# Graph attention on one Trainium2 core: value blocks of three batches in the setup and the rest in batch 3, a value step moved, narrow flag and input-sum products

## The chip, the cores and the metric

The kernel runs on one core of a Trainium2 chip. The core has five engines that run side by side, each with a stream of instructions of its own: TensorE (PE in the profile, its weight loads PEld) multiplies matrices, VectorE (DVE), ScalarE (ACT) and GpSimd (POOL) work on elements, SyncE (SP) does nothing here but issue transfers. The metric is the time of one execution on the device in microseconds (us); less is better.

## The reference

One layer of graph attention with 16 batches (B), 512 rows each (N), 512 features (F), 16 heads of 32 and 20 keys (the first 20 rows). All is float32. Cut to what matters:

```python
row_zero = v.sum(-1) == 0
q_exp = jnp.where(row_zero[..., None], 0.0, q[:, None, :])
self_feat = concatenate([v, q_exp], -1) @ W_self.T + b_self      # (16, 512, 512)
output = self_feat
for d in range(2):
    A = adj if d == 0 else swapaxes(adj, 1, 2)                   # (16, 512, 512, 11) int
    A = A[:, :, :20]
    cond, vb = A.sum(-1), A @ w_bias + b_bias
    kv = self_feat[:, :20]
    qh = (self_feat @ Wq[d].T + bq[d]).reshape(B, N, 16, 32)
    kh = (kv @ Wk[d].T + bk[d]).reshape(B, 20, 16, 32)
    aff = einsum('bnhd,bmhd->bnhm', qh, kh) / sqrt(32)
    w = softmax(where(cond[:, :, None] > 0, aff, -9e15) + vb[:, :, None])
    out_t = einsum('bnhm,bmf->bnhf', w, kv)
    output = output + (einsum('bnhf,hgf->bnhg', out_t, Wout[d]) + bout[d]).reshape(B, N, F)
out = v + relu(output)
```

## The kernel before, in words

The order of the instructions on every engine is the order in which they are written: the kernel turns the automatic scheduler off and interleaves the work by hand. Tiles come from pools; a new tile of a pool waits until the one that held its place is done with.

**What is computed.** The query projection is folded into the keys: for each key row and head the kernel makes one vector over the 512 features, so that the scores of a tile of 128 rows and all 16 heads, two directions and 19 keys (key 0 is taken off the others) are a product of the row features with 608 columns. In the same way the output weights are folded into the values ("vw": for each batch 20 rows by 512 for each direction). The weighted sum then needs the values of four heads laid out in blocks, zero outside, so that one product does several heads.

**Setup (lines 458 to 786).** In this order:
- All loads are issued at once, most on SP's queue in the order of lines 511 to 529 (`wo_sb`, the output weights, come after the first `x`, line 527), the first ones on ACT's.
- `kv_terms` (line 537): the features of the 20 key rows of all batches, 320 columns, as the sum over four chunks k of the input for each of four chunks fc of features: 16 products 128 x 128 x 320 (`ps_kv`). The first two rounds of k are written ahead of the products with `q` (line 547), the third and fourth behind them. A product with `ones` over a sum of the inputs gives the flags of zero rows of the keys (line 555).
- `key_rows` (line 589): the 304 columns of key differences `kvD` by the key weights, eight groups (d, jc), each over four chunks k as four products of 32 outputs (line 596), one for each quarter of the 128 output partitions. The first four groups come ahead of the bursts, the others with the first bursts. DVE adds the bias (line 602), into `khD`.
- Twenty **bursts** (line 745). A burst makes the folded keys (`keys`, line 672) for 26 or 25 units; its products (line 681) go to a pair of PSUM tiles from `ps_s`, of which there are two, so each burst waits until ACT (line 696) and DVE (line 698) have read the one before. Finished stages are written to DRAM (`g_d`, `g1_d`, lines 703 and 704) and read back per batch.
- Between the bursts stand fillers from a table (`plan`, line 726): each word is the list of fillers behind one burst, counted from the burst at which the key rows are all made. `m` is a bias term, `v` a value step, `w` a value step of the last 64 rows, `b` and `c` biases, `n` the flags of zero rows of batches 0 and 1 (`row_flags`, line 211: one product of 128 x 128 ones with 512 columns), `p` one of the seven block products for the features of batch 0. Ahead of burst n = 4 stands one value step outside the table (line 749).
- A **value step** (`values`, line 645) is one chunk k of the product of key features with output weights: for the first 256 rows (t = 0, 1) four products of 32 outputs over 512 columns. Behind the fourth chunk DVE copies the sum out (line 660) and POOL issues transfers to `vw_d` in DRAM (line 664), split at batch `EARLY` into two parts of their own.
- `bd_d`, also in DRAM in two parts, holds the **value blocks**. Part 0 is zeroed by one transfer on POOL's queue (`clear_first`, line 145), part 1 by eight on SP's (`clear_rest`, line 153, issued in batches 0 to 2 at the places `clears(b)`). Then `blocks` (line 161) lists twelve transfers for each part, each of which copies runs of 128 bytes from `vw_d` to `bd_d`, and `spill(n, queue)` (line 184) issues the next n of them. Part 0: six on POOL's queue behind the late bursts (line 774), six in batch 0 (line 871).

**The loop (line 806).** For each batch b four tiles nt of 128 rows. Per tile: `scores` (line 349, products at line 365) on TensorE; `weigh` (DVE: add, maximum, subtract, lines 379 to 387); `expo` (ACT, line 392); in the next tile `normal` (DVE sum and reciprocal, lines 415 and 416, POOL product, line 417) and `turn` (DVE, line 424). In the third tile of batch b the weighted sum of batch b - 1 is made (`attend`, line 435, `ps_o`), with its values loaded from `bd_d` in tile 0 (`load_values`, lines 137 and 850), and DVE, ACT and POOL finish it (lines 441 to 449).

Beside that the next batch is prepared: its features by seven block products (`product`, line 250; DVE puts the parts together in `partial`, line 285, and `joined`, line 297), differences of its inputs on POOL (`x_sum`, line 233), masks (ACT lines 317 and 337, DVE line 328, POOL line 344), and the sums of rows (`row_sum`, line 189, on ACT, tile 3 of batch b for batch b + 2), from which come the flags of zero rows (`nz`). Block products 4 and 3 of batch b come in its own tile 0, around the scores: the first half of these scores (k = 0, 1, line 837) stands ahead of `partial(b, 1, 0)` on DVE, the second half (k = 2, 3, line 844) behind it.

**SP's queue.** SP issues nearly all loads of the loop, in written order: `load_x` (107), `load_xn` (113), `load_adj` (119), `load_cq` (124), `load_keys` (135), `load_values` (141), `load_nz` (202), the stores (454). Most are held back until a named instruction of another engine is done (`behind`, line 97), so that a pool's place is free and loads come in turn. Part 1 of the value blocks is copied from here: four places in a batch, each with `spill(1)` in batches 3, 4 and 5 (lines 856, 877, 909, 932): behind the mask load of tile 0, behind `x_sum` 1 and its mask load, behind `x_sum` 2 in tile 1, and in tile 2 behind two pieces of `load_xn` and ahead of the last (line 939).

Of the kernel before, what the change touches and what calls it, by code (L numbers as in the profile page):

```python
# [13 lines left out]
P = 128  # L14
# [4 lines left out]
def gat_kernel(  # L19
# [20 lines left out]
    nc = tc.nc  # L40
# [42 lines left out]
    cq_d = dram.tile([B, H, 2, NG], F32, name="cq_d")  # L83
    EARLY = 5
    parts_of = ((0, EARLY), (EARLY, B))
# [98 lines left out]
    def spill(n, queue=nc.sync):  # L184

        for _ in range(n):
            queue.dma_start(*copies.pop(0))
# [23 lines left out]
    def row_flags(b):  # L211
        ps = bank(f"ps_nz{b}")
        nc.tensor.matmul(ps[:, :N], ones, rss[b], start=True, stop=True)  # L213
        nzs[b] = load.tile([P, N], F32, tag="nz", name=f"nz{b}")
        nc.vector.tensor_scalar(nzs[b], ps[:, :N], 0.0, None, ALU.not_equal)
# [242 lines left out]
    with tc.tile_pool(name="setup", bufs=1) as sp, tc.tile_pool(name="ps_acc", bufs=4, space=PSUM) as acc["pool"]:  # L458
# [19 lines left out]
        with tc.tile_pool(name="setup_k", bufs=1) as sk:  # L478
# [58 lines left out]
            def kv_terms(fc, k):  # L537
                nc.tensor.matmul(  # L538
                    kv_ps[fc][:, :BM], ws_v[:, k, bass.ts(fc, P)], xkv[:, k],
                    start=(k == 0), stop=(k == C - 1),  # L540
                )

# [80 lines left out]
        with tc.tile_pool(name="setup_g", bufs=4) as sg:  # L623
# [101 lines left out]
            }  # L725
            plan = "mmvv bvv vvc vvc vvn vvw vvw vw wn p p p p p p p".split()

# [17 lines left out]
            for n, runs in enumerate(bursts):  # L745
                for i in range(len(rest)):
                    if (i < 1 and n > 0) or any(fc == 0 and (d, hg) == rest[0] for fc, hg, d, _, _ in runs):
                        key_rows(*rest.pop(0))
                if n == 4:
                    values(*steps["v"].pop(0)[1])  # L750
# [44 lines left out]
    with tc.manual_schedule():  # L795
# [10 lines left out]
        for b in range(B):  # L806
# [7 lines left out]
            for nt in range(NT):  # L814
# [13 lines left out]
                if nt == 0:  # L828
# [4 lines left out]
                    else:  # L833
# [38 lines left out]
                    if more:  # L872
                        x_sum(b + 1, 1)
                        load_adj(b + 1, 0, done["xsum"], slice(1, 2))
                        clears(b)
                        if b in (3, 4, 5):
                            spill(1)
                    else:
# [3 lines left out]
                if nt == 1:  # L882
# [21 lines left out]
                    if more:  # L904
                        x_sum(b + 1, 2)
                        load_adj(b + 1, 1, done["xsum"], slice(1, 2))
                        clears(b)
                        if b in (3, 4, 5):
                            spill(1)
                        x_sum(b + 1, 3)  # L910
# [5 lines left out]
                if nt == 2:  # L916
# [6 lines left out]
                    if b > 0:  # L923
# [4 lines left out]
                        if b + 2 < B:  # L928
                            load_xn(b + 2, 0, done["add", 1], slice(1, 2))
                            load_xn(b + 2, 1, done["add", 3], slice(0, 1))  # L930
                            if b in (3, 4, 5):
                                spill(1)
                    else:
# [161 lines left out]
```

## Time and profile before

| what | value |
|---|---|
| three timed runs | 580.28, 582.24 and 582.8 us, median 582.24 |
| the profiled execution | 581.09 us |
| its span in the profile | 579.3 us |
| mean granted clock of TensorE | 0.998 |
| DVE, ACT, POOL busy | 492.8, 393.8, 405.5 us |
| moved from and to HBM | 82.30 MB read, 40.24 MB written |

The span is the time from the first to the last instruction in the profile; the 1.8 us around it are the rest of the execution. Busy time is the sum of an engine's instructions, without waits. The chain of waits follows the work that ended last back to the start, from each instruction to what released it. An arrow `<-` behind an idle time names what ended it. In a row of the timeline stand start, length, engine, line and operation, and a figure in brackets is the wait ahead of it.

### The profile page before, as it was taken

What the parts mean: (1) busy time and instruction counts of PE and PEld (TensorE: products, weight loads), DVE (VectorE), ACT (ScalarE), POOL (GpSimd) and SP (SyncE); (2) the same over time, 40 slices, a digit from 0 to 9 for tenths busy, and PEclk for the clock granted to TensorE, in tenths of its full rate; (3) what the DMA queues carried; (4) which work ended last, traced back from release to release, by engine and by line L of the source; (5) the groups of instructions that cost most, each with busy time, mean ns of one, the idle gap of its engine ahead of it and who ended that gap; (6) DMA issues with size and microseconds to landing.
All of it is one profiled execution on the core that took longest, in us unless ns stands there. A gap on an engine that the chain in (4) does not pass through costs nothing.

```text
span 579.3 us, 30986 instructions
## 1 busy us (share of the span) xinstructions
PE 572.1 (99%) x13496; PEld 434.0 (75%) x13496; DVE 492.8 (85%) x790; ACT 393.8 (68%) x1162; POOL 405.5 (70%) x383
## 2 busy tenths in 40 slices
PE   9999999999999999999999999999999999999996
PEld 6544458888878787878778787887887878787873
DVE  0685676979898989898999999898989898989896
ACT  1234554587878777778786868687887877777571
POOL 2636977648686776858585867786858677786874
PEclk9999999999999999999999999999999999999999
DMA  8999998757776777778576767576666766664404
GB/s 287 386 405 311 335 363 290 210 144 220 210 233 183 207 203 201 215 178 235 169 217 168 219 168 209 165 216 179 203 197 188 202 195 182 194 202 111 146 19 147
DMA packets 98787, 123.26 MB, mean 213 GB/s; under 512 B 18876, under 2 KB 66968, under 8 KB 96604
## 3 DMA queue, kind: packets, MB, share of 16 engines
q1 hardware_dynamic: 96124, 117.80, 66.2%
q0 software_dynamic: 1392, 2.43, 1.8%
q8 instruction: 106, 1.74, 1.3%
q10 hardware_dynamic: 1136, 1.06, 0.5%
q14 instruction: 29, 0.24, 0.1%
HBM read 82.30 MB, written 40.24 MB: 212 GB/s over the span
## 4 chain that ended last, share of the span: by engine, by line
PE 97%; DMA 1%; DVE 0%; issue 0%; SPq 0%; DVEq 0%
PE ps_s L365 46%; PE ps_a L283 19%; PE ps_c L283 9%; PE ps_o L435 6%; PE ps_d L283 5%; PE ps_v L654 3%; PE ps_k L596 3%; DMA ws_q<-in_wsT 1%; PE ps_o L798 1%; PE ps_kv L538 0%; PE ps_nz L213 0%; PE ps_s L354 0%; PE _g(0, 2, 0, 14, 16)0_440 L681 0%; PE _g(2, 2, 0, 14, 16)0_836 L681 0%; PE _g(1, 2, 0, 14, 16)0_644 L681 0%
## 5 line engine op out<-in xcount | busy, mean ns | idle before, releaser
L365 PEld LDWEIGHTS ps_s<-g,sf 128*32 128x32 f32 x8192 | 263.1, 110 | 21.8 <-issue 14.7
L365 PE MATMUL ps_s<-g,sf 128*32 128x152 f32 x8192 | 277.4, 293 | 0.7 <-issue 0.7
L337 ACT COPY both<-add 32x80 f32<-32x80 f32 x512 | 130.9, 256 | 61.0 <-DVE add L328 55.1
L417 POOL TENSOR_TENSOR s<-s,sm 128x640 f32<-128x640 f32 x63 | 80.4, 1276 | 96.0 <-DVE sm L416 73.5
L344 POOL TENSOR_TENSOR full<-cq,both 128x640 f32<-128x640 f32 x64 | 100.4, 1569 | 26.8 <-issue 20.9
L317 ACT ACTIVATE prod<-adj,wb_sb 128x80 f32<-128x80 int32 x330 | 112.4, 431 | 0.0
L392 ACT ACTIVATE s<-s 128x640 f32<-128x640 f32 x63 | 46.5, 738 | 55.4 <-DVE s L387 55.0
L449 POOL TENSOR_TENSOR o<-o,x 128x512 f32<-128x512 f32 x60 | 76.3, 1293 | 0.0
L379 DVE TENSOR_TENSOR full<-ps_s,full 128x608 f32<-128x608 f32 x63 | 48.7, 773 | 21.6 <-PE ps_s L365 19.0
L415 DVE TENSOR_REDUCE sm<-s 128x32 f32<-128x640 f32 x63 | 50.8, 806 | 10.7 <-ACT s L392 10.5
L283 PE MATMUL ps_a<-t,ws_s 128*32 128x246 f32 x1024 | 59.4, 371 | 0.0
L383 DVE TENSOR_REDUCE ps_s<-full 128x32 f32<-128x640 f32 x63 | 52.2, 828 | 2.2
L424 DVE STREAM_TRANSPOSE wt<-s 128x640 f32<-128x640 f32 x63 | 52.7, 837 | 0.6 <-POOL s L417 0.6
L387 DVE TENSOR_TENSOR s<-full,ps_s 128x640 f32<-128x640 f32 x63 | 51.5, 817 | 1.1
L289 DVE SCALAR_TENSOR_TENSOR sf<-nz,qw,ps_a 128x246 f32<-128x246 f32 x128 | 51.5, 442 | 0.2
L283 PEld LDWEIGHTS ps_a<-t,ws_s 128*32 128x32 f32 x1024 | 34.2, 110 | 16.7 <-issue 0.6
L328 DVE TENSOR_REDUCE add<-prod 128x80 f32<-128x960 f32 x32 | 36.8, 1149 | 7.2 <-ACT prod L317 7.2
L446 ACT ACTIVATE o<-o,bo 128x512 f32<-128x512 f32 x60 | 38.3, 710 | 0.6 <-DVE o L444 0.6
L248 POOL TENSOR_TENSOR t<-x,t 128x492 f32<-128x492 f32 x32 | 36.8, 1151 | 1.3
L248 POOL TENSOR_TENSOR t<-x 128x492 f32<-128x492 f32 x32 | 36.9, 1154 | 0.0
L435 PE MATMUL ps_o<-wt,vd 32*32 32x512 f32 (+5 forms) x816 | 36.8, 578 | 0.1
L444 DVE TENSOR_TENSOR o<-ps_o,sf 128x512 f32<-128x512 f32 x60 | 36.7, 668 | 0.0
(225 smaller groups left out, 715.4 us busy)
## 6 DMA issues: line engine op xcount, KB each, us to landing
g<-g_d SPq DMA_DIRECT2D x60, 304.0 KB
g_d<-st SPq DMA_DIRECT2D x16, 1064.0 KB
out_T<-o SPq DMA_DIRECT2D x60, 256.0 KB
xn<-in_xn SPq DMA_DIRECT2D x56, 256.0 KB
x<-in_xT SPq DMA_DIRECT2D x56, 256.0 KB
adj<-in_adj SPq DMA_DIRECT2D x60, 220.0 KB
nz<-nz_d SPq DMA_DIRECT2D x14, 256.0 KB
wk<-in_wkT SPq DMA_DIRECT2D x2, 1024.0 KB
```

Of the source, the lines that this page charges most:

```text
L248: done["xsum"] = nc.gpsimd.tensor_sub(t, one, two)
L283: nc.tensor.matmul(to, lhs, x[:, k], start=start, stop=stop, skip_group_check=n != 2)
L289: done["partial"] = nc.vector.scalar_tensor_tensor(to[:, i], nzs[b][:, half(l)], qw[:, 2 * f + i, b : b + 1], parts[b, "a"][i][:, :HN], AL ...
L317: nc.scalar.activation(p[:, :, l], a[:, :, l], AF.Identity, scale=wb_sb[:, l : l + 1])
L337: done["spread"] = nc.scalar.copy(adds[b, h][bass.ts(a, R), :, g], add[r].rearrange("p (t m) -> p t m", t=2))
L344: done["full"] = nc.gpsimd.tensor_add(f, cqs[b].unsqueeze(1).to_broadcast(shape), adds[b, nt // 2][:, nt % 2].unsqueeze(2).to_broadcast(sh ...
L365: nc.tensor.matmul(to, sfs[b][:, k, bass.ds(nt * P + (2 * g + j) * R, R)], of, start=(onto is None and k == 0 and (whole or j == 0)), stop ...
L383: nc.vector.tensor_reduce(mx, f, AX.X, ALU.max)
L417: done["normal"] = nc.gpsimd.tensor_mul(s, s, sm.unsqueeze(3).to_broadcast(full))
L424: nc.vector.transpose(wts[b][:, nt], s.rearrange("p a h m -> p (a h m)"))
L435: nc.tensor.matmul(banks[a][bass.ds(at // 2 * DH, n * DH)].rearrange("p (t n) -> p t n", n=32), vd[r, bass.ds(at * DH, n * DH)], wt[r, :, ...
L449: nc.gpsimd.tensor_add(o[:, c], o[:, c], xs[b][:, c])
```

## The change

- `EARLY` goes from 5 to 3. Part 0 of the value blocks holds batches 0 to 2, part 1 batches 3 to 15. Sizes of transfers follow: `vw_d` is split at row 60 in place of 100, `clear_first` writes three runs a partition in place of five, each `clear_rest` 104 rows in place of 88, and of the twelve copies of a part those of part 0 go over 3 batches in place of 5, those of part 1 over 13 in place of 11.
- The twelve copies of part 1 are all issued in batch 3, three at each of the four places, in place of one at each place in batches 3, 4 and 5.
- `row_flags`: four products with 32 outputs each in place of one with 128, over the same 512 columns, twice.
- `kv_terms`: each of the 16 products becomes four with 32 outputs.
- One value step more stands outside the table, ahead of burst n = 3; the seventh word of the table has one `v` fewer.

```diff
-    EARLY = 5
+    EARLY = 3
...
     def row_flags(b):
         ps = bank(f"ps_nz{b}")
-        nc.tensor.matmul(ps[:, :N], ones, rss[b], start=True, stop=True)
+        for a in range(HL):
+            nc.tensor.matmul(ps[bass.ts(a, R), :N], ones[:, :R], rss[b], start=True, stop=True)
...
             def kv_terms(fc, k):
-                nc.tensor.matmul(
-                    kv_ps[fc][:, :BM], ws_v[:, k, bass.ts(fc, P)], xkv[:, k],
-                    start=(k == 0), stop=(k == C - 1),
-                )
+                for a in range(HL):
+                    nc.tensor.matmul(
+                        kv_ps[fc][bass.ts(a, R), :BM], ws_v[:, k, bass.ds(fc * P + a * R, R)], xkv[:, k],
+                        start=(k == 0), stop=(k == C - 1),
+                    )
...
-            plan = "mmvv bvv vvc vvc vvn vvw vvw vw wn p p p p p p p".split()
+            plan = "mmvv bvv vvc vvc vvn vvw vw vw wn p p p p p p p".split()
...
-                if n == 4:
+                if n in (3, 4):
                     values(*steps["v"].pop(0)[1])
                 keys(runs)
...
-                        if b in (3, 4, 5):
+                        if b == 3:
                             copies = copies or blocks(1)
-                            spill(1)
+                            spill(3)
```

The same edit of `spill(1)` to `spill(3)`, in batch 3 alone, stands at the other three places.

More of the change, by code (lines that the diff above doesn't have):

```diff
@@ L875, in gat_kernel @@
                         clears(b)
-                        if b in (3, 4, 5):
-                            spill(1)
+                        if b == 3:
+                            spill(3)
                     else:
@@ L907, in gat_kernel @@
                         clears(b)
-                        if b in (3, 4, 5):
-                            spill(1)
+                        if b == 3:
+                            spill(3)
                         x_sum(b + 1, 3)
@@ L930, in gat_kernel @@
                             load_xn(b + 2, 1, done["add", 3], slice(0, 1))
-                            if b in (3, 4, 5):
-                                spill(1)
+                            if b == 3:
+                                spill(3)
                     else:
```

## The prediction

> **What bounds the kernel now.** I read the busy line and the chain of the page first, then the chain row by row, then the engines' timelines around the places that the change touches.
>
> ```profile
> PE 572.1 (99%) x13496; PEld 434.0 (75%) x13496; DVE 492.8 (85%) x790; ACT 393.8 (68%) x1162; POOL 405.5 (70%) x383
> PEclk9999999999999999999999999999999999999999
> PE 97%; DMA 1%; DVE 0%; issue 0%; SPq 0%; DVEq 0%
> ```
>
> TensorE is busy all the time, at full granted clock in every slice, and 97% of the chain that ends last is its own work. So a saving counts only if it takes time from TensorE, and a loss counts as soon as something makes TensorE wait. The chain row by row shows how even the batches are (start, length; the row is the weighted sum that comes once in each batch):
>
> ```profile
> 190.03 2.17 PE ps_o L435 x48
> 220.51 2.17 PE ps_o L435 x48
> ...
> 281.46 2.17 PE ps_o L435 x48
> 311.94 2.17 PE ps_o L435 x48
> ```
>
> The stretch 190.03 to 220.51, which holds block copies (line 187) of batches 3 and 4, takes 30.48 us; 281.46 to 311.94, which has none, takes 30.48 too. So copies spread one by one over batches 3, 4 and 5 cost nothing, and taking them out of batches 4 and 5 brings nothing. What is left to ask is what setup gains, and what batch 3 makes of twelve.
>
> **The change, part by part.**
>
> *Flags (line 213), twice.* PE's timeline in setup (start, length):
>
> ```profile
> 35.58 0.30 PE L681 MATMUL _g(0, 2, 0, 14, 16)0_440<-khD,wq_sb 32*128 32x38 f32 x2
> ...
> 37.02 2.25 PE L596 MATMUL ps_k<-kvD,wk 128*32 128x304 f32 x32
> ...
> 52.74 0.30 PE L681 MATMUL _g(1, 2, 0, 14, 16)0_644<-khD,wq_sb 32*128 32x38 f32 x2
> ...
> 53.91 1.92 PE L654 MATMUL ps_v<-wo_sb,kvT 128*32 128x512 f32 x16
> 55.77 1.13 PE L213 MATMUL ps_nz<-rx,ones 128*128 128x512 f32 x2
> 56.82 0.41 PE L681 MATMUL s_g(1, 3, 0, 7, 16)0_683<-khD,wq_sb 32*128 32x171 f32 x2
> ```
>
> The wide flag product holds TensorE from 55.77 to 56.82, 1.05 us for 512 columns. Two groups of four 32-output products over the same 512 columns (line 654, 16 records) hold it from 53.91 to 55.77, so 0.93 us each. Gain 0.12 us each, 0.24 us for both flags. Ends: nothing, and 0.4 us if a group right behind a value step costs less than the mean of two.
>
> *Input sums (line 538), sixteen products made into 64.* From PE's timeline and from the chain:
>
> ```profile
> 11.31 2.39 PE L538 MATMUL ps_kv<-xkv,ws_v 128*128 128x320 f32 x8
> ```
> ```profile
> 26.92 2.18 PE ps_k L596 x32
> ```
>
> Four wide products (two records each) take 2.39 us, about 0.60 us for 320 columns. The key rows are groups of four narrow products over 304 columns; 32 records are four groups, 0.545 us each, which is 0.57 us for 320 columns. That is 0.03 us a product and I count nothing; ends 0.1 us either way, since only the last two rounds lie on the path. The Trainium skill speaks against this edit: TensorEngine Tiling (Array Packing), section Instruction Overhead, gives each matmul some 60 cycles of overhead. At the 2.4 GHz of TensorE: Matmul & The Clock Gate, 48 added products of two passes each would be an estimated 2.4 us slower if they queued; the key rows above, where narrow products cost no more per column than wide ones, do not bear that out.
>
> *Value step ahead of the fourth burst (n = 3).* That burst lasts from 35.58 to 37.02, 1.44 us; the burst of the same shape at 52.74 lasts until 53.91, 1.17 us. The difference, 0.27 us, is its wait for the last key rows, which DVE frees late:
>
> ```profile
> 35.94 0.59 DVE L602 TENSOR_SCALAR khD<-ps_k,bk_sb 128x304 f32<-128x304 f32 x1
> ```
>
> DVE ends at 36.53. With a value step of 0.93 us in front, the burst starts near 36.5 and the wait is gone; the step itself is only moved, since the plan has one fewer later. Gain 0.27 us; from it goes what DVE loses when a value copy comes a burst earlier, up to 0.2 us. Is the weight there? SP, and the POOL sum that waits for the first x:
>
> ```profile
> 14.21 0.56 SPq L107 DMA_DIRECT2D x<-in_xT  x1
> ...
> 23.13 1.99 SPq L500 DMA_DIRECT2D wo_sb<-in_woT  x2
> ```
> ```profile
> 27.33 1.29 POOL L207 TENSOR_TENSOR rx<-x 128x512 f32<-128x512 f32 x1 [3.64 <-DMA x<-in_xT]
> ```
>
> A load of that size issued at 14.21 was there at 27.33, 13.1 us. The first half of wo_sb, issued at 23.13, would then be there at 36.2 at the latest, and the step wants it near 35.6: a wait of 0 to 0.6 us. I take 0, as the queue ahead of it is shorter by then.
>
> *Blocks of three batches in setup.* The same number of copies and clears is issued, each with less in it. On POOL the six copies that stand ahead of batch 0's first normalisation get shorter at most, and behind them POOL waits for DVE anyway:
>
> ```profile
> 99.71 1.27 POOL L417 TENSOR_TENSOR s<-s,sm 128x640 f32<-128x640 f32 x1 [1.50 <-DVE sm L416]
> ```
>
> So nothing. Setup in all: 0.24 + 0.27 = 0.5 us faster; ends 0.9 us faster and 0.5 us slower.
>
> *Twelve copies in batch 3, three at each of four places.* SP's queue there:
>
> ```profile
> 186.12 0.88 SPq L187 DMA_DIRECT2D bd_d<-vw_d  x1
> 187.11 1.04 SPq L119 DMA_DIRECT2D adj<-in_adj  x1
> 188.20 0.81 SPq L187 DMA_DIRECT2D bd_d<-vw_d  x1
> 189.13 1.73 SPq L202 DMA_DIRECT2D nz<-nz_d  x1
> 190.96 1.76 SPq L124 DMA_DIRECT2D cq<-cq_d  x4
> 192.82 0.85 SPq L119 DMA_DIRECT2D adj<-in_adj  x2
> 193.72 1.52 SPq L187 DMA_DIRECT2D bd_d<-vw_d  x1
> 195.34 1.42 SPq L113 DMA_DIRECT2D xn<-in_xn  x3
> 196.81 0.78 SPq L187 DMA_DIRECT2D bd_d<-vw_d  x1
> 197.69 0.53 SPq L113 DMA_DIRECT2D xn<-in_xn  x1
> ```
> ```profile
> 278.44 1.66 SPq L202 DMA_DIRECT2D nz<-nz_d  x1
> ```
>
> From 186.12 to 198.22 SP issues for 11.32 of 12.10 us: with four copies the queue is nearly full. Eight more stand ahead of the last xn piece. Upper end: 8 x 1.0 us (the mean of the four copies here) less the 0.78 us of gaps, 7.2 us late. Lower end: everything at its shortest, 12 copies of 0.80, 12 loads of 0.4 and 24 gaps of 0.05, is 15.6 us from 186.12, 201.7 instead of 198.2, 3.5 us late. I take 4.8 us: the lower end and the 1.3 us by which the nz load is long in batch 3 and, without any copy near, in batch 6.
>
> Who waits for that piece? ACT's row sums, in order with all else of ACT:
>
> ```profile
> 202.72 0.63 ACT L193 ACTIVATE xn<-xn 128x512 f32<-128x512 f32 x1 [0.15 <-DMA xn<-in_xn]
> ...
> 205.06 4.26 ACT L337 COPY both<-add 32x80 f32<-32x80 f32 x16 [1.62 <-DVE add L328]
> 209.35 0.74 ACT L392 ACTIVATE s<-s 128x640 f32<-128x640 f32 x1
> ```
>
> Already now the last row sum waits 0.15 us for its piece. Behind it ACT has 1.62 us of slack ahead of the 16 spreads, then none: spreads, then the exponential of the last tile. Behind ACT comes DVE, and behind DVE comes TensorE:
>
> ```profile
> 210.12 0.82 DVE L415 TENSOR_REDUCE sm<-s 128x32 f32<-128x640 f32 x1 [0.57 <-ACT s L392]
> ...
> 211.24 0.75 DVE L289 SCALAR_TENSOR_TENSOR sf<-nz,qw,ps_a 128x246 f32<-128x246 f32 x2
> ```
> ```profile
> 210.58 4.13 PE ps_s L365 x128
> ```
>
> DVE waits for that exponential, then makes the last part of batch 4's features (line 289, until 211.99), and the second half of batch 4's first scores, from 210.58 + 2.07 = 212.65, multiplies them: 0.66 us of slack. In all 1.62 + 0.66 = 2.3 us. TensorE then stands for 4.8 - 2.3 = **2.5 us**, once; afterwards every engine is late by the same. Ends: 3.5 - 2.3 = 1.2 and 7.2 - 2.3 = 4.9 us; if also the landing is quicker behind a later issue, nothing. The keys of batch 4, queued behind that piece, have until 210.58 and later, and the value blocks of batch 3 are loaded in batch 4, behind all of these: both wanted later than what waits above.
>
> **Sum.** -0.5 + 2.5 = +2.0 us. The profiled execution took 581.09 us, 579.3 of it span: 583.1. The three timed runs have a median of 582.24, and the mean of the four is 581.6; I put the sum on that: **583.6 us**.
>
> **The rivals.**
>
> *The copies fit.* If the last piece comes less than 2.3 us late, because SP has more idle time than I see or the piece lands faster after its issue, TensorE never waits: 581.6 - 0.5 = 581.1. For it: the row sum waits only 0.15 us now. Against it: even the shortest issue times make 3.5 us.
>
> *The queue gives way to the copies.* One of the four copies above took 1.52 us to issue. If one in each group of three does, and the loads between stay as long as in batch 3, then 4 x (1.52 + 2 x 0.82) = 12.6 us of copies, 7.3 of loads and 1.2 of gaps make 21.1 us in place of 12.1: the piece is 9.0 us late and TensorE stands for 6.7 us in the same place, 581.6 - 0.5 + 6.7 = 587.8, slower. It decides from where the piece is 5.7 us late (a stall of 3.4 us, a net loss of 2.9). For it: four copies in 12 us fill the queue now. Against it: in three of four cases a copy's issue stayed below 0.9 us.
>
> *A long stall also cools TensorE.* The weight loads of the first input sums, 5 us after the start:
>
> ```profile
> 4.82 0.34 PEld L538 LDWEIGHTS ps_kv<-xkv,ws_v 128*128 128x128 f32 x1 [0.20 <-issue]
> 5.35 0.34 PEld L538 LDWEIGHTS ps_kv<-xkv,ws_v 128*128 128x128 f32 x1 [0.20 <-issue]
> ```
>
> They come 0.53 us apart, where the round at 11.31 takes 2.39 us for eight, 0.30 each: near half pace, some 4 us after the first product. If a stall of 4.0 us brought that pace back for 4 us, about 1.8 us would go on top: 581.6 - 0.5 + 4.0 + 1.8 = 586.9. For it: the pace at the start. Against it: the stall must be long, and the clock row shows no dip to read it from. The Trainium skill has a rule that would do this: TensorE: Matmul & The Clock Gate, Part 1, says that after an idle window of about 3.4 us the clock is halved, and that it comes back after a busy one as long. The slow start agrees with it; no stall of that length is in this trace.
>
> *The narrow products and the moved step do not do what they are for.* If neither shortens TensorE, and the stall comes, 581.6 + 2.5 = 584.1; with the wait for wo_sb 584.7.
>
> **How the numbers follow.** Forecast (a stall of 1 to 3.4 us, with the gain of setup or without) 0.50, of which the rival in which the products and the step bring nothing has 0.12; copies fit 0.17; queue gives way 0.19; cooled 0.08; a gain in setup that I do not see, over 3 us, 0.06. The difference that a measurement of this kernel can tell from none is about 0.5%, 2.9 us: faster 0.06, same 0.50 + 0.17 = 0.67, slower 0.19 + 0.08 = 0.27. The range goes from 580.6 (copies fit, near setup's best end) to 587.0 (cooled, and the lower half of the queue's case); what lies outside has about 0.17.
>
> **What would show it.** In the profile after: the flag products a little over 0.9 us apart from their neighbours and the burst at n = 3 near 1.17 us; SP's row of the last xn piece in batch 3 at 201 to 205 instead of 197.69; ACT's row sums there with a wait of several us for xn; the first scores of batch 4 split in the chain by DVE, with one batch of about 33 us among batches of 30.48. If that batch is also 30.48, the stall is wrong. If setup ends (first scores of batch 0) later than before, the gain is wrong.

## The result, and the profile after

The changed kernel takes 589.77 us (median of five runs, 587.56 to 590.35), the kernel before 581.79 us (five runs, 579.79 to 582.80): 1.0128 times as long, 95% interval 1.0105 to 1.0151. It is 8 us slower; the forecast was 583.6, and its range ended at 587.0. The profiled execution took 589.77 us, its span is 587.5 us, 8.2 more than before.

The page of the kernel after has the lines that were first shown of before:

```profile
PE 575.0 (98%) x13604; PEld 431.1 (73%) x13604; DVE 493.0 (84%) x790; ACT 394.0 (67%) x1162; POOL 404.0 (69%) x383
PEclk9999999999999999999999999999999999999999
PE 62%; DMA 1%; POOL 0%; DVE 0%; ACT 0%; SPq 0%; issue 0%; DVEq 0%
```

TensorE is still busy for 98%. The chain has 62% of TensorE where it had 97%, but the shares here add up to 63%: this chain is followed back only to 206.65 us, and the 35% of the span before that are not in it. Its first piece is

```profile
206.65 2.50 POOL o L450 x2
```

and from 218.92 us to the last products it is TensorE's. So the chain leaves TensorE at one place, between 206.65 and 218.92, and says nothing of what lies earlier. The rows that come once in a batch tell where the time went (TensorE's timeline: start, length; the weighted sums made in batches 2, 3 and 4):

```profile
160.66 2.24 PE L436 MATMUL ps_o<-wt,vd 32*64 32x512 f32 x48
...
191.14 2.24 PE L436 MATMUL ps_o<-wt,vd 32*64 32x512 f32 x48
...
228.50 2.24 PE L436 MATMUL ps_o<-wt,vd 32*64 32x512 f32 x48
```

From 160.66 to 191.14 are 30.48 us, as before; from 191.14 to 228.50 are 37.36 us. Batch 4 is 6.89 us longer than the 30.47 before (189.97 to 220.44 in the same view), and every later batch takes 30.47 or 30.48 again. The rest lies in setup. Before, the first burst started at 25.80 and the first scores of batch 0 at 90.48, 64.68 us apart. After:

```profile
26.21 0.53 PE L683 MATMUL s_g(0, 0, 0, 0, 16)0_369<-khD,wq_sb 32*128 32x304 f32 x2
...
92.28 11.94 PE L366 MATMUL ps_s<-g,sf 128*32 128x152 f32 x364
```

66.07 us, 1.39 more. The sum: 0.41 (the first burst starts later) + 1.39 - 0.62 (batch 0, in which TensorE's waits for nothing that the profile shows are shorter) - 0.01 + 6.89 = 8.06 of the 8.2 us.

**Batch 4.** TensorE's timeline, with its waits in brackets:

```profile
212.79 0.47 PE L366 MATMUL ps_s<-g,sf 128*32 128x152 f32 x8 [1.04 <-DMA g<-g_d]
213.55 2.02 PE L366 MATMUL ps_s<-g,sf 128*32 128x152 f32 x56 [0.29 <-DMA g<-g_d]
218.92 3.86 PE L366 MATMUL ps_s<-g,sf 128*32 128x152 f32 x64 [3.35 <-DVE sf L290]
```

The first half of the first scores waits 1.04 and 0.29 us for the keys (`g`), the second half 3.35 us for DVE's line 290 (289 before). Then 64 products take 3.86 us, where 128 take 4.13 elsewhere. The table by stretches gives the granted clock of the stall and of what follows it (length, busy time of PE, PEld, DVE, ACT, POOL, then PEclk):

```profile
215.60:218.90 3.30, 0.00 (x0) 0.00 (x0) 1.50 (x4) 3.24 (x11) 1.72 (x2) 0.98 0.77 269
218.90:222.80 3.90, 3.88 (x68) 2.98 (x72) 3.06 (x4) 2.59 (x10) 3.71 (x5) 0.58 0.62 193
```

0.58 behind the stall: TensorE runs at half pace for most of these 3.9 us. The page's clock row, one digit for 14.7 us, shows nothing of it. In the other four runs of this kernel the mean granted clock points the same way: 0.992 to 0.996 in three that took 589.43 to 590.35 us, 1.000 in the one that took 587.56.

Now back from the stall, as the prediction had it. SP's queue, ACT and DVE:

```profile
186.24 2.25 SPq L119 DMA_DIRECT2D adj<-in_adj  x1
188.53 2.60 SPq L187 DMA_DIRECT2D bd_d<-vw_d  x3
191.24 0.49 SPq L119 DMA_DIRECT2D adj<-in_adj  x1
191.77 2.71 SPq L187 DMA_DIRECT2D bd_d<-vw_d  x3
194.59 0.52 SPq L202 DMA_DIRECT2D nz<-nz_d  x1
195.21 2.48 SPq L124 DMA_DIRECT2D cq<-cq_d  x4
197.79 0.84 SPq L119 DMA_DIRECT2D adj<-in_adj  x2
198.69 2.45 SPq L187 DMA_DIRECT2D bd_d<-vw_d  x3
201.24 2.44 SPq L113 DMA_DIRECT2D xn<-in_xn  x3
203.74 2.42 SPq L187 DMA_DIRECT2D bd_d<-vw_d  x3
206.26 1.66 SPq L113 DMA_DIRECT2D xn<-in_xn  x1
```
```profile
211.71 0.63 ACT L193 ACTIVATE xn<-xn 128x512 f32<-128x512 f32 x1 [4.20 <-DMA xn<-in_xn]
...
212.34 4.24 ACT L338 COPY both<-add 32x80 f32<-32x80 f32 x16
216.60 0.74 ACT L393 ACTIVATE s<-s 128x640 f32<-128x640 f32 x1
```
```profile
217.37 0.82 DVE L416 TENSOR_REDUCE sm<-s 128x32 f32<-128x640 f32 x1 [6.64 <-ACT s L393]
...
218.49 0.76 DVE L290 SCALAR_TENSOR_TENSOR sf<-nz,qw,ps_a 128x246 f32<-128x246 f32 x2
```

The last xn piece is issued until 207.92 in place of 198.22. The last row sum starts at 211.71 behind a wait of 4.20 us, in place of 202.72; batch 3 itself began 1.17 us later (191.14 against 189.97), so it is 7.82 us late. The spreads, the exponential and DVE follow without a gap, DVE after 6.64 us of waiting. It is the chain of engines that the prediction named. The profile's own chain of waits names another releaser for the spreads, the keys' load at 210.76; which of the two it is, an experiment below decides.

**Setup.** POOL before, where its eight cq_d transfers do not wait for one another or for others, and the mask product follows at 58.78:

```profile
56.25 2.52 POOL L640 DMA_DIRECT2D cq_d<-c  x4 [0.29 <-POOL c L638]
58.78 2.11 POOL L314 TENSOR_TENSOR prod<-prod,wb_sb 128x880 f32<-128x880 f32 x1
```

POOL, DVE and TensorE after, ahead of burst n = 11:

```profile
57.78 1.87 POOL L642 DMA_DIRECT2D cq_d<-c  x3 [0.29 <-POOL c L640]
61.51 0.62 POOL L642 DMA_DIRECT2D cq_d<-c  x1 [1.86 <-DMA vw_d<-v]
62.15 2.12 POOL L315 TENSOR_TENSOR prod<-prod,wb_sb 128x880 f32<-128x880 f32 x1
...
66.17 0.58 POOL L324 TENSOR_SCALAR prod<-cond 128x80 f32<-128x80 f32 x1
```
```profile
66.78 1.15 DVE L329 TENSOR_REDUCE add<-prod 128x80 f32<-128x960 f32 x1 [2.58 <-POOL prod L324]
```
```profile
69.30 0.46 PE L683 MATMUL s_g(2, 1, 1, 4, 16)1_854<-khD,wq_sb 32*128 32x228 f32 x2 [1.18 <-DVE st L700]
```

POOL's last cq_d transfer waits 1.86 us for a vw_d transfer ahead of it; the mask product behind it starts at 62.15 (58.78 before), DVE waits 2.58 us for POOL's part of the mask, and the burst waits 1.18 us for DVE. None of these three waits was there before.

### The profile page after: what moved, and what is told of

Its sections match the earlier page's. It is cut to its first block, busy times and chain, and to the rows that moved or that the text cites. A ratio compares the mean times of both kernels' runs of the same rounds, so it can differ in the third digit from the quotient of the medians.

```text
span 587.5 us, 31205 instructions
## 1 busy us (share of the span) xinstructions
PE 575.0 (98%) x13604; PEld 431.1 (73%) x13604; DVE 493.0 (84%) x790; ACT 394.0 (67%) x1162; POOL 404.0 (69%) x383
## 4 chain that ended last, share of the span: by engine, by line
PE 62%; DMA 1%; POOL 0%; DVE 0%; ACT 0%; SPq 0%; issue 0%; DVEq 0%
PE ps_s L366 34%; PE ps_a L284 12%; PE ps_c L284 7%; PE ps_o L436 5%; PE ps_d L284 3%; DMA g<-g_d 1%; PE ps_o L800 1%; POOL o L450 0%; PE ps_s L355 0%; DVE sm L416 0%; SPq L455 0%; ACT both L338 0%; ACT s L393 0%; DVE o L1034 0%; SPq L135 0%
## 5 line engine op out<-in xcount | busy, mean ns | idle before, releaser
L193 ACT ACTIVATE xn<-xn 128x512 f32<-128x512 f32 x56 | 34.4, 615 | 7.7 <-DMA xn<-in_xn 7.7
```

## The experiments

Three numbers are taken of each kernel, from TensorE's timeline: the time from the first burst to the first scores (setup), the length of batch 4 (from one weighted sum to the next), and, where it was timed, the ratio to the kernel before with its 95% interval. Both lengths are those of one profiled execution; a kernel without a ratio was executed once.

| kernel | setup, us | batch 4, us | ratio |
|---|---|---|---|
| before | 64.68 | 30.47 | |
| after | 66.07 | 37.36 | 1.0128 (1.0105 to 1.0151) |
| setup_only | 64.26 | 30.48 | 1.0006 (0.9995 to 1.0018) |
| step_only | 64.67 | 30.48 | |
| narrow_only | 64.28 | 30.53 | |
| blocks_only | 66.57 | 35.45 | 1.0120 (1.0100 to 1.0139) |
| sums_late | 64.48 | 32.56 | 1.0088 (1.0062 to 1.0114) |
| copies_8 | 66.27 | 31.25 | |
| copies_small | 65.69 | 30.48 | |
| warm_fill | 64.87 | 35.69 | 1.0104 (1.0075 to 1.0134) |
| vw_sp | 64.29 | 36.80 | |
| copies_pool | 65.65 | 32.24 | 1.0044 (1.0027 to 1.0061) |
| fixed | 64.31 | 32.78 | 1.0026 (1.0014 to 1.0039) |
| early4 | 64.72 | 30.47 | |
| pieces_60 | 64.68 | 30.48 | |
| pieces_64 | 64.99 | 30.48 | |
| pieces_68 | 66.45 | 30.48 | |
| pieces_62 | 73.75 | 30.47 | |
| edge_64 | 64.68 | 37.59 | |
| best | 64.28 | 30.48 | 0.9974 (0.9962 to 0.9985) |

### The parts of the change

**setup_only**: the change without its blocks (`EARLY = 5`, one copy at a place in batches 3, 4 and 5).

> Narrow flag and input-sum products and the moved value step, with the value blocks as before (five batches in setup, one copy at a place in batches 3, 4 and 5). Theory: the loss of 8 us in the profile after has two places, batch 4 (6.9 us: PE stands 5.1 us and then runs 64 products in 3.86 us in place of 2.07) and setup (burst n = 11 waits for DVE, 1.8 us longer, because POOL's last cq_d transfer waits for the vw_d transfer of the moved step). Then batch 4 takes 30.5 us again and what is left is setup: with the POOL wait it is 0 to 1.5 us slower than before, ratio 1.000 to 1.003. Rival one (the wait on POOL comes from the split at row 60, not from the step): no wait on POOL, burst n = 11 takes 1.04 us as before, 0.5 to 1 us faster, ratio 0.998 to 0.999. Rival two (the loss in batch 4 comes from setup, through everything being late): batch 4 stays near 37 us and the ratio near 1.012.

Batch 4 is whole, and the kernel takes the same time as before. Burst n = 11 has no wait, and POOL waits for no transfer among its cq_d transfers: rival one held, not the theory. Its gain did not come, though: setup is 0.42 us shorter in the profile, but the timed ratio shows none. The wait on POOL belongs to the split, not to the step.

**blocks_only**: the kernel before with `EARLY = 3` and `spill(3)` in batch 3.

> Value blocks of three batches, twelve copies in batch 3, all else as before. Theory: the twelve copies alone make batch 4 about 37.4 us long (6.9 more than 30.48), with PE's second half of the first scores at half pace, and setup is as before: 6.5 to 7 us slower, ratio 1.011 to 1.012. Rival (setup and copies add up in batch 4, by loads that are late already): less than 4 us slower, ratio under 1.007.

Nearly the whole loss is here. Batch 4 is 4.98 us longer, less than the 6.9 expected: after a wait of 3.02 us for DVE the second half runs at full pace (PEclk 1.00, 2.40 us in the row of the timeline). Setup was expected as before and is 1.89 us longer: POOL waits 2.82 and 0.23 us among its cq_d transfers.

```profile
216.00:219.00 3.00, 0.00 (x1) 0.01 (x1) 1.52 (x4) 2.95 (x10) 1.74 (x2) 1.00 0.85 308
219.00:221.40 2.40, 2.40 (x68) 2.12 (x72) 2.15 (x4) 2.03 (x7) 2.21 (x4) 1.00 0.58 189
```

**step_only** and **narrow_only**: the kernel before with the moved value step alone, and with the narrow products alone.

> The moved value step alone (split at row 100, wide products). Theory: the value step's sum is ready one burst earlier, so both its vw_d transfers stand ahead of all eight cq_d transfers on POOL's queue, and the eighth cq_d transfer waits for the second of them: 0.5 to 2 us of wait on POOL, DVE's mask sum (the row that was at 63.08) 1.5 to 3.5 us later, burst n = 11 0.4 to 1.8 us longer; ahead of that burst n = 3 is 0.27 us shorter. In all setup ends 0 to 1.5 us later than before. Rival (the size of the second transfer, 68 rows in place of 28, is what makes it late): no wait of POOL for a transfer, setup ends 0.2 to 0.4 us earlier.

Rival, again: POOL does not wait. But the step gains nothing either, 64.67 us. The wait at burst n = 3 is gone (1.18 us from 36.26 to 37.44, 1.44 before), and burst n = 6, behind the value copy that now comes a burst earlier on DVE, takes 1.40 us in place of 1.12.

> Narrow flag and input-sum products alone. Theory: each flag product 0.2 us shorter (0.4 in all), the last two rounds of input sums about 0.2 us earlier, but the key rows then wait for wk (0.43 us in the profile after), so that of the input sums nothing is left: the first scores of batch 0 come 0.2 to 0.6 us earlier than 90.48, unless the load of wk itself comes later in that execution. Rival (narrow products cost an overhead for each): the last two rounds of input sums take over 2.6 us each in place of 2.4, setup ends later.

The flags bring 0.40 us, in burst to scores 64.28. The input sums bring nothing: their last two rounds take 2.36 us each, against 2.39 and 2.40 of the wide ones. In this execution the key rows did not wait for wk; in five of the seven others with narrow input sums they waited 0.4 to 1.0 us for it, so what these rounds might gain is the load's to give.

### The stall of batch 4

**sums_late**: the changed kernel, with the row sums of batch 3 behind the exponential.

```diff
-                    if 0 < b < B - 2:
+                    if 0 < b < B - 2 and b != 3:
                         for j in range(4):
                             row_sum(b + 2, j)
...
-                    if b == 0:
+                    if b in (0, 3):
                         for j in range(4):
-                            row_sum(2, j)
+                            row_sum(b + 2, j)
```

> The changed kernel, with the four row sums that ACT makes in batch 3 (for batch 5) put behind the exponential of the last tile, as batch 0 has them. Theory: TensorE's stall of 3.35 us in batch 4 is the wait of these sums for the last xn piece, handed on by the 16 spreads, the exponential and DVE. With the sums behind, DVE has the exponential in time, and what is left in batch 4 is the keys' own lateness (1.0 and about 0.7 us in the profile after): batch 4 takes 30.5 to 32.5 us in place of 37.4, with no products at half pace, and the kernel is 2 to 4 us slower than before, ratio 1.003 to 1.007. Rival (the keys' load, which the chain of waits names, sets the end in any order of ACT): batch 4 stays above 35 us, ratio 1.010 or more.

DVE's wait is gone, and with it the slow half; what is left are the keys' own waits:

```profile
213.46 0.47 PE L366 MATMUL ps_s<-g,sf 128*32 128x152 f32 x8 [0.29 <-DMA g<-g_d]
215.30 2.02 PE L366 MATMUL ps_s<-g,sf 128*32 128x152 f32 x56 [1.38 <-DMA g<-g_d]
```

32.56 us: in this profile 4.8 us of the 6.89, the half pace among them, were handed on by ACT's row sums, and 2.1 are left, in which the keys, queued on SP behind the same copies, are waited for. So the link from the keys to the spreads in the profile's chain is not what held DVE. The time says less: the ratio is above what was expected (1.003 to 1.007) and below the rival's 1.010, and its interval overlaps that of after. The profiled execution was the shortest of the six (584.12 us, the longest 588.96); part of its lead is setup, 64.48 us, and what the others lost beyond it stays open.

**copies_8** and **copies_small**: blocks alone, with two copies a place (four of the twelve left out), and with twelve copies of one batch's runs each (`bd_d[n][:, 0]` and the same of `vw_d` in place of all thirteen batches).

> Blocks alone (all else as before), with two copies at each of the four places of batch 3; the other four copies are left out, so that part of the value blocks of batches 3 to 15 stay zero. Theory: lateness goes with the number of copies ahead of the last xn piece, 4 more than before in place of 8: the piece is 3.7 to 4.2 us late, less 2.3 of slack is a stall of 1.4 to 1.9 us, and batch 4 takes 31.9 to 32.6 us; nothing at half pace. Rival (the queue breaks down only beyond some filling): no stall, 30.5 us. Rival (a wait of another kind that three copies set off and two also do): above 34 us.

```profile
207.15 0.63 ACT L193 ACTIVATE xn<-xn 128x512 f32<-128x512 f32 x1 [1.82 <-DMA xn<-in_xn]
```

The last row sum is 207.15 - (202.72 + 1.47 of later start) = 2.96 us late, and batch 4 is 0.78 us longer, where 1.4 to 1.9 were expected. So there are 2.2 us of slack; with twelve whole copies (blocks_only: 7.36 us late, 4.98 longer) 2.4. The stall grows with the lateness beyond the slack; that the lateness here is less than half that of twelve was not foreseen.

> Blocks alone, twelve copies in batch 3, but each copies one batch's runs (4 x rows) in place of thirteen's (52 x rows), so that the value blocks of batches 4 to 15 stay zero. If what makes the last piece late is the number of transfers that SP issues, it is as late as with whole copies, 8.3 us at its issue, and batch 4 takes 35 to 37.4 us. If it is the runs of 128 bytes that the queue has to work off (by which the loads between take 10.7 us to issue in place of 7.3), copies and loads are short again: the piece is at most 5 us late, batch 4 takes 30.5 to 33 us.

```profile
198.26 1.83 SPq L190 DMA_DIRECT2D bd_d<-vw_d  x3
200.19 0.40 SPq L113 DMA_DIRECT2D xn<-in_xn  x1
```

No stall: the last piece is issued until 200.59. From the first copy to there SP takes 13.3 us; in blocks_only, with the same number of transfers, 20.6 (187.66 to 208.26). A copy takes 0.61 us to issue in place of 0.92, and the six groups of loads between them 5.1 us in place of 8.8. So it is not the number of transfers that fills the queue but what each copy moves: its runs of 128 bytes and with them its bytes, which this run does not tell apart.

**copies_pool**: the changed kernel, the twelve copies issued by POOL (`spill(3, nc.gpsimd)`).

> The changed kernel, with the twelve copies of batch 3 at the same places, issued by POOL in place of SP. Theory: the stall of batch 4 comes from SP's queue, in which the loads stand behind the copies. With SP free the last xn piece and the keys come on time, batch 4 takes 30.5 to 31.5 us, and the kernel is 0.5 to 2 us slower than before by its setup, ratio 1.001 to 1.004. Rival one (the DMA engines themselves are filled by the runs of 128 bytes, on whatever queue): the last xn piece lands 4 us late or more, batch 4 takes 33 to 37 us. Rival two (12 x 0.65 us of issue on POOL make its sums and products late): a stall of over 1 us behind POOL in batch 3 or 4.

SP is free and the last xn piece is there in time, but rival two holds:

```profile
184.06 2.54 POOL L187 DMA_DIRECT2D bd_d<-vw_d  x3
...
207.04 0.56 POOL L324 TENSOR_SCALAR prod<-cond 128x80 f32<-128x80 f32 x1
```
```profile
208.82 4.26 ACT L338 COPY both<-add 32x80 f32<-32x80 f32 x16 [3.11 <-DVE add L329]
```

Four times 2.5 us of issue make POOL late: its part of the mask comes at 207.04 (202.46 before), and the spreads wait 3.11 us for DVE, which waits for it. Batch 3 takes 31.78 us, batch 4 32.24. With all twelve copies in batch 3, the queue that is taken decided who was late; on either of the two something was.

**warm_fill**: the changed kernel, with 32 more products between the two halves of the first scores of batch 4.

```diff
+                        if b == 4:
+                            fill(b)
                         for g in range(2):
                             scores(b, nt, g, ps[g], range(2, C))
```

> The changed kernel with 32 more block products (two passes, some 3.3 us) on TensorE in batch 4, between the two halves of the first scores, into a PSUM tile that nobody reads any more. Theory: they lie in the stall of 3.35 us, and since TensorE then hardly stands, the second half of the scores takes 2.07 us in place of 3.86: batch 4 is up to 1.8 us shorter than after's 37.4, the kernel 0 to 1.8 us faster than after, ratio to before 1.009 to 1.013. Rival (the slow second half has another cause, the keys or DVE): it takes over 3 us again. Rival (the stall is not idle time that can be filled): batch 4 is 3.3 us longer, ratio 1.018.

```profile
217.54 3.50 PE L290 MATMUL ps_d<-x,ws_v 128*32 128x246 f32 x64
220.86 2.25 PE L375 MATMUL ps_s<-g,sf 128*32 128x152 f32 x64
```

The 64 records of added work lie in the stall, and the second half follows at full pace (next row at 222.93, 2.07 us later). Batch 4 is 1.67 us shorter than in the profile of after. The times alone do not tell the two kernels apart, as their intervals overlap.

### The transfer of 68 rows

**vw_sp**: the changed kernel, the vw_d transfers of the first 128 rows on SP's queue.

> The changed kernel, with the vw_d transfers of the first 128 value rows (both directions, split at row 60) issued by SP in place of POOL. Theory: what the split costs in setup is POOL's wait for a transfer ahead in its queue, handed on by the mask product on POOL and the mask sum on DVE to burst n = 11. With these transfers on another queue POOL does not wait among the cq_d transfers, burst n = 11 takes 1.04 us as before, and the first scores of batch 0 start at 89.8 to 90.8, as in the kernels split at row 100 (90.2 to 90.5), in place of 91.3 to 92.7. Batch 4 stays long (35 to 37.4 us). Rival (the split delays DVE or PE by another way): first scores after 91.3.

64.29 us, and POOL's eight cq_d transfers follow one another (from 55.59 on four in 2.48 us). The setup part of the loss is this wait: in the four other profiles with the moved step and the 68 rows on POOL's queue (sums_late, warm_fill, copies_pool, after) POOL waits 0.28, 0.68, 1.42 and 1.86 us for them, and setup is 0.22, 0.61, 1.39 and 1.81 us longer than in setup_only. Batch 4 stays long, with a wait of 3.29 us for DVE and a clock of 0.58 behind it.

**fixed**: vw_sp and copies_pool together.

> Both of these edits: the first vw_d transfers on SP's queue, the twelve copies on POOL's. Theory: both losses are gone, and what is left of the change is the gain of its setup edits: within 1.5 us of before, ratio 0.998 to 1.003, first scores at 89.8 to 90.8 and batch 4 30.5 to 31.5 us. Rival: either loss stays, ratio 1.004 or more.

Setup is whole, batch 4 is not (2.3 us longer), for POOL's reason: the spreads wait 3.11 us for DVE, as in copies_pool. The rival held. 1.5 of the 8 us stay.

**early4**: the kernel before with `EARLY = 4`, copies 2, 1, 2 and 1 at the four places of batches 3 and 4.

> The kernel before with blocks of four batches in setup (split at row 80), the twelve copies at two, one, two, one a place in batches 3 and 4. Theory: two copies more than before ahead of the last xn piece make the last row sum about 1.5 us late, less than the 2.6 us of slack: batches 4 and 5 take 30.5 us each. In setup, if it is any split that leaves over 64 or about 64 rows for the second transfer that is slow, row 80 (48 rows) starts the first scores at 90.2 to 90.6; if every split but that at 100 is slow, at 91.3 to 92.7. Rival (slack is used up already with six copies): a batch of over 31 us.

Setup as before, and batch 4 too; batch 5 takes 30.77. Six copies fit, and not because slack absorbs them. The last row sum was expected 1.5 us late and is not late at all, since SP's queue takes no longer than with four:

```profile
185.65 1.32 SPq L187 DMA_DIRECT2D bd_d<-vw_d  x2
...
197.05 0.59 SPq L113 DMA_DIRECT2D xn<-in_xn  x1
```

From the first copy to the end of the last xn piece are 11.99 us, against 12.10 before (a copy has 48 x rows runs here and 44 before); best, below, which has the same copies, takes 12.21. Eight copies take 15.4 us (copies_8), twelve 19.2 to 21.5 in the six profiles that have them whole on SP's queue. Why the stretch begins to grow between six and eight, no run here tells.

Row 80 costs nothing. What is it then with row 60? **pieces_60**, **pieces_64** and **edge_64** cut a transfer in two, for example

```diff
-                        for n, lo, hi in ((0, 0, edge), (1, edge, rows)) if t == 0 else ((1, 0, rows),):
+                        for n, lo, hi in ((0, 0, 60), (0, 60, edge), (1, edge, rows)) if t == 0 else ((1, 0, rows),):
```

> The kernel before, with the vw_d transfer of its 100 rows cut in two at row 60 (three transfers for each of the first two value sums; blocks as before). If the cut at row 60 makes the transfers late, those that start or end at row 60 land 7 us or more after their issue, POOL waits among the cq_d transfers, and the first scores start 65.2 us or more after the first burst, in place of 64.7. If it is the blocks of three batches in another way, they land after 4 to 6 us and it stays at 64.7.

> As pieces_60, cut at row 64. If the place of the cut decides, no transfer is late, 64.7 us. If three transfers in place of two are themselves the cause of lateness, as late as pieces_60.

> Blocks alone (split at row 60, twelve copies in batch 3), with the second transfer of 68 rows cut at row 64 into 4 and 64 rows. If it is the 68 rows from row 60 on that are slow, the wait on POOL is gone: 64.7 us from the first burst to the first scores in place of 65.7 to 66.6; batch 4 stays at 35 to 37.4 us. If the cut at row 60 is slow in any form, over 65.2.

Neither cut is slow by itself (64.68 and 64.99), and with the 68 rows cut into 4 and 64 the wait of POOL is gone. So it is the transfer of 68 rows: its place or its number of rows.

> The kernel before, with the vw_d transfer of 100 rows cut at row 68 (68, 32 and 28 rows). Theory: 68 rows spread over few DMA engines, so 68 rows from row 0 on are late too: about 7 us or more from issue to landing, 32 rows 4 to 6 us. By the Trainium skill, DMA: Bandwidth & Descriptors, section Why a DMA increments its semaphore by 16 and not by 1, a transfer runs on the largest number of engines up to 16 that divides its rows; that is 4 for 68, 16 for 32 and 14 for 28. Rival (it is the place, rows 60 to 127, that is slow): 68 rows from row 0 land after 4 to 6 us.

> The kernel before, with the vw_d transfer of 100 rows cut at row 62 (62, 38 and 28 rows), beside pieces_60 (60, 40 and 28), whose pieces landed after 4.5, 5.2 and 4.8 us. Theory: 62 and 38 rows divide still worse than 68, so both land later than the 60 and 40: 8 us or more for 62 rows, POOL waits among the cq_d transfers, and from the first burst to the first scores it takes over 65 us in place of 64.7. By the page of the Trainium skill named for pieces_68 both would run on 2 engines. Rival (the place or the mere number of transfers): 4 to 6 us as in pieces_60.

The number, in one execution each. The view of the transfers gives KB each and the median from issue to landing, for POOL's queue in setup; 2 KB are one row. The kernel before with its 100 rows, after with 68 and 60 rows, then the kernel before cut at row 68 and at row 62:

```profile
vw_d<-v POOLq DMA_DIRECT2D x2, 200.0 KB, 5.2
```
```profile
vw_d<-v POOLq DMA_DIRECT2D x2, 136.0 KB, 7.6
vw_d<-v POOLq DMA_DIRECT2D x2, 120.0 KB, 4.5
```
```profile
vw_d<-v POOLq DMA_DIRECT2D x2, 136.0 KB, 7.8
```
```profile
vw_d<-v POOLq DMA_DIRECT2D x2, 124.0 KB, 15.1
vw_d<-v POOLq DMA_DIRECT2D x2, 76.0 KB, 13.4
```

68 rows take 7.6 and 7.8 us here, wherever they start, 62 rows 15.1, while 100 rows took 5.2 and 60 rows 4.5. The figures spread: over the seven profiles with 68 rows on POOL's queue from row 60 on, they land after 6.5 us (sums_late, the smallest loss) to 8.2 (blocks_only, the largest wait of POOL), and transfers of 64 rows took up to 7.7 (warm_fill). The 62 rows stand far outside that. Behind a late transfer the next ones are late too (the 38 rows, 13.4 us, and of a number that was not late before, 28 rows, 14.2). With 62 rows POOL waits so long that setup takes 73.75 us. The Trainium skill, DMA: Bandwidth & Descriptors, section Why a DMA increments its semaphore by 16 and not by 1, says that a transfer runs on the largest number of engines up to 16 that divides the slowest dimension of both its sides, here the rows: 4 for 68, 2 for 62 and 38, but 10 for 100, 15 for 60, 16 for 80, 64 and 48. The trace agrees with the order of 62, 68 and the rest. It does not show the engines of a transfer, and the page names an exception for some direct copies, so that the number of engines is the reason is argued, not shown.

### A version that is faster

**best**: early4 with the narrow flag products.

> Blocks of four batches (six copies in each of batches 3 and 4, as in early4) and narrow flag products, nothing else. Theory: 64.3 us from the first burst to the first scores, batches 4 and 5 30.5 to 30.8 us, so about 0.4 us less than before at best: ratio 0.998 to 1.001, which a measurement of this kernel can hardly tell from no change. Rival (six copies use up the slack in some executions): ratio over 1.002.

0.9974 (0.9962 to 0.9985), 580.44 us against 582.35: faster than both kernels, by more than was expected. The span is 577.9 us, 1.4 less than in the profile before: 0.40 in setup, 0.29 by an earlier first burst, and 0.62 in batch 0, where before TensorE waited 0.15 and 0.59 us for nothing that the profile shows, and here it does not. Such waits were 0 to 2.5 us in these kernels without a pattern that the runs explain; so only 0.40 us of the gain is shown to come from the edit.

## Why the prediction was wrong

- **The bound** was right: copies in batches 4 and 5 cost nothing, and without them these batches gain nothing. So nothing could be won there.
- **Flags**: forecast 0.24 us, measured 0.40. **Input sums**: nothing forecast, nothing found, and no loss either. The estimate of 2.4 us that the prediction took from the Trainium skill, TensorEngine Tiling (Array Packing), section Instruction Overhead, is not in the trace: it would be 0.6 us a round, and a round takes 2.36 us against 2.39 and 2.40.
- **Value step**: the gain of 0.27 us came at its burst (0.26), and the loss on DVE that stood beside it with "up to 0.2" came too (0.28). The value taken, 0.27, was the end without the loss; net nothing.
- **"Blocks of three batches in setup ... So nothing"** failed. It counted transfers, which stay as many, and bytes, which go down; it did not ask what a split at row 60 makes of the two transfers of a value sum. The one of 68 rows lands after 7.6 us, and POOL hands its wait on. Price: 1.81 us in the profile after (1.39 with the gains of setup taken off), and 0.2 to 1.9 us in the seven profiles that have this transfer on POOL's queue, each against the kernel with the same products and without it. The rows of before had no transfer that was late in this way, and the bound "at most shorter" had no second side.
- **Twelve copies: "I take 4.8 us: the lower end"** failed, and it is the largest error. From the first copy to the end of the last piece SP takes 19.4 us in after and 20.6 in blocks_only, against 15.6 for the lower end, in which loads shrink to 0.4 us each. They did not: 8.4 and 8.8 us for twelve loads, not 4.8, and more than the 7.3 of before. That is 7.3 and 8.5 us longer than before's 12.1, at the upper end of 7.2 or above it. The lower end's loads were seen in copies_small alone, 5.1 us, where the copies are small. Nor does the cost grow evenly, as both ends took it to: from four copies to six it is nothing, behind that 1.2 to 1.7 us for each.
- **Slack of 2.3 us and the chain of engines** were right: 2.2 and 2.4 by the length of batch 4 in copies_8 and blocks_only. By the start of the second half of the scores it is 2.7 in blocks_only and in after, as TensorE starts behind the first of DVE's two parts. Sized rightly, 7.4 - 2.3 gives the 5 us of blocks_only.
- **Keys "wanted later than what waits above"** was wrong. TensorE waits for them in the first half of the scores, 1.04 and 0.29 us in after and 2.04 and 1.49 us in edge_64, whose DVE then costs only 0.41 us more; in sums_late they are what is left. In after DVE's end hides them. So moving the row sums alone does not mend batch 4.
- **The cooled rival**, at 0.08, happened on top: price forecast 1.8 us, measured 3.86 - 2.07 = 1.79. That these agree is partly luck. The pace was read from the start of the kernel, and there the profile gives a granted clock of 1.00 (4.20 to 8.00 us of before): by that record the start was slow for another reason, which stays open, and it is no instance of the rule. It and "the queue gives way" were priced as alternatives, 586.9 and 587.8, each on a kernel with nothing else wrong. But a late queue is what makes the stall long: they come together. The lateness forecast by the second, 9.0 us, was near the 7.8 of after; its reason (copies of 1.52 us) was not, as a copy took 0.85 us there on the mean.
- Put together from measured terms: -0.4 for the flags, +1.8 for the split, +5.1 for the stall, +1.8 for half pace are 8.3 us; the timed difference is 8.0. The terms come from single profiles, so that they meet to 0.3 us says no more than that nothing large is missing.

## What to carry to other kernels

Do not price additions to a queue that issues for 11.3 of 12.1 us at everything's shortest: two more transfers cost nothing here, and each further one 1.2 to 1.7 us to everything behind it, which only runs with different numbers of them showed. Look for the in-order engine that waits for the last of them. Before a transfer's size is changed, look at how its number of rows divides, not only at its bytes. Rivals that share a cause are added, not set side by side.

## What the runs showed of the hardware

- Behind waits of 3.35 us (after) and 3.29 us (vw_sp) the granted clock over the next 3.9 us was 0.58; behind one of 3.02 us (blocks_only) it was 1.00. In edge_64 two waits of 2.04 and 1.49 us, with eight products between them, were followed by 0.50. The rule of the Trainium skill that the prediction named, TensorE: Matmul & The Clock Gate, Part 1, puts the idle window at about 3.4 us; the waits of after and vw_sp agree within 0.15 us, and edge_64 shows half pace with no single wait of that length. No length that is always safe is shown: three other executions of blocks_only have a mean granted clock of 0.991 to 0.994, where the kernel before has 0.997 to 1.000.
- SP's time to issue a load depends on what was queued ahead of it: the same twelve loads took 8.8 us among copies of 52 x rows runs and 5.1 us among copies of 4 x rows.
- The same twelve loads and the copies among them take SP 12.1 us with four copies, 12.0 and 12.2 with six, 15.4 with eight and 19.2 to 21.5 with twelve.
- The number of a transfer's rows can matter more than its bytes: 62 rows took 15.1 us to land, 100 rows 5.2, in the same place of setup.
